# A transformer block with causal attention: softmax sums from four added key tiles instead of two, and the projection's weights loaded and gated later

## The chip, the core and the metric

The kernel runs on one core of a Trainium2 chip. The core has a matrix engine (TensorE, PE in the profile), two vector engines (VectorE, DVE; GpSimd, POOL), an engine for activation functions (ScalarE, ACT) and a queue that issues most of the loads and stores (SyncE, SP). Each engine takes its instructions in order, and waits for others by semaphores. The metric is the device time of one execution in microseconds (us), the median of some runs.

## The reference

x is 2 batch rows x 2048 tokens x 512; the condition is 2 x 512; 16 heads of 32; all in float32.

```python
mod = silu(condition) @ Wada + bada
sh_a, sc_a, gt_a, sh_m, sc_m, gt_m = split(mod, 6, axis=1)
xm = layernorm(x, g1, be1) * (1 + sc_a) + sh_a
q, k, v = split_heads(xm @ Wqkv)
scores = where(causal, q @ k.T * hd ** -0.5, -inf)
att = softmax(scores) @ v                       # per head, then merged
x = x + gt_a * (att @ Wproj + bproj)
xm = layernorm(x, g2, be2) * (1 + sc_m) + sh_m
x = x + gt_m * (gelu(xm @ W1 + b1) @ W2 + b2)
```

## The kernel before

The work goes row by row: QKV of row 0, attention of row 0, the projection of row 0 with the beginning of QKV of row 1, QKV and attention of row 1, the projection of row 1, and then the MLP over both rows.

**Units and steps.** The 16 heads are four groups c of four heads (HC = 4). A unit is one group and one block i of 512 queries: 16 units for each row, in the order i = 0, 1, 2, 3 for the first group and 0, 2, 1, 3 for the others; the last one, unit 15, is (c = 3, i = 3). A unit's steps are its key tiles of 128: 4i full steps, and then three masked ones (widths 512, 384 + 128 and 256). So a unit of i = 3 has 15 steps, one of i = 0 has 3.

**A step** (`scores_t`, L444) makes transposed scores, keys on the partitions, queries along the row, in four PSUM banks `st`, one for each head. Each bank first takes the product `st<-fold,sel`, which puts minus the row maximum into it, and then adds the product of keys and queries. ScalarE's exponential of each bank is the tile `e` (12 buffers, three steps). In a masked step GpSimd clears the upper triangle with `affine_select` (L487). Two steps later (LAG = 2) TensorE multiplies e with the values into `o` (four heads side by side, 32 columns each) and, for the softmax's denominator, with a matrix of ones into `sm`.

**Sums.** Full steps do not multiply each e with ones. GpSimd adds the e of an even and the following odd step, head by head (`pair_sums`, L504 to L508, the tiles `ee`, EE_BUFS = 6), and the set of four products with ones of that sum is put into the list `pending` for LAG + 1 = 3 steps after the odd step (L632 to L639). Masked steps multiply their e directly. `flush(now)` at the end of each step's scores emits what is due. `finish` (L517) copies o and sm, sends the sums through a reciprocal and DRAM (r, rd, rb) and multiplies (`ot` times `rb`, L540, on VectorE).

**Maxima ahead.** The row maxima must be known before a unit begins. In the same steps TensorE therefore makes the plain scores of units up to two ahead (`row.score`, tiles `s` in two PSUM banks, and once in a step a borrowed `st` bank), and VectorE reduces each tile to its maximum (L363, or L358 for masked tiles). How many tiles a step makes is paced by the cost list `weight` (L563) and the function `due` (L566). When a unit's last tile is reduced, `split` (L366) writes the maxima as a high and a low part into `mhl` (a cast at L377 and a subtraction at L378), and `rows` (L414) transposes them (`ps_m`) and makes `fold` from them. The last unit has no tiles left to make.

**Before the projection.** `prefetch` (L313), called in step 3 of the last unit, takes the buffer `kst0` of the finished keys and loads into it two blocks of attention output (`at_s`), four tiles of x (`xt_s`) and the four tiles that the next stage needs first (`next_s`). The projection's weights `wproj` and its bias `bgate` have buffers of their own. `gate_weights` (L817) loads them in the QKV stage of the same row, broadcasts the gate of the condition with one product (`rows_of`) and multiplies it into bgate and the four parts of wproj on VectorE. `project_phase` (L826) adds bgate to each tile of x on GpSimd (L849), multiplies with wproj, adds and stores.

**Order.** A scheduler places the instructions on each engine's queue by their order in the program and by when it reckons their inputs and buffers ready. Instructions wrapped in `mm`, `transpose` or `act` keep the program's order on their engine: all products, and ScalarE's work in attention. GpSimd's and VectorE's work and the loads on SP may be moved, within their dependences. A pool with `bufs` buffers hands out whichever is free.

Of the kernel before, what the change touches and what calls it, by code (L numbers as in the profile page):

```python
# [8 lines left out]
F32 = mybir.dt.float32  # L9
# [3 lines left out]
ALU = mybir.AluOpType  # L13
# [14 lines left out]
def dit_block_kernel(  # L28
# [33 lines left out]

    nc = tc.nc
# [12 lines left out]
    EE_BUFS = 6  # L76
# [66 lines left out]
    wproj = bp.tile([P, C, D], F32, tag="wproj", name="wproj")  # L143
# [62 lines left out]
    def rows_of(psum, r, b):  # L206

        ps = psum.tile([P, D], F32, tag="mm", name="ps_rows")
        g = slice(r * HD, (r + 1) * HD)
        mm(ps, pick[g, b, :], modr[g, :], start=True, stop=True)  # L210
        return ps
# [57 lines left out]
    class Row:  # L269
# [42 lines left out]

        def prefetch(self):  # L313

# [11 lines left out]
            self.next_s = [  # L326
                st[:, (3 * C + n) * QB : (3 * C + n + 1) * QB] for n in range(TQ)
            ]
            b = self.b
            nc.sync.dma_start(self.at_s[0], od[b][last_order[0]])  # L330
# [7 lines left out]
            nc.sync.dma_start(self.at_s[1], od[b][last_order[1]])  # L338

# [97 lines left out]
    def attention_phase(row):  # L437
        b, vv, kst, qst = row.b, row.vv, row.kst, row.qst
        with pool(f"att{b}") as ap, pool(
# [4 lines left out]
            def scores_t(u, step, n):  # L444
# [26 lines left out]
                for h in range(HC):  # L471
# [11 lines left out]
                    if tiles[0][0] >= i * TQ:  # L483
# [3 lines left out]
                        nc.gpsimd.affine_select(  # L487
                            d, d, pattern=[[0, len(tiles)], [1, P]],
                            compare_op=ALU.is_ge, fill=0.0,
                            base=0, channel_multiplier=-1,  # L490
# [13 lines left out]
            def pair_sums(es0, es1):  # L504
                out = new_sums()
                for h in range(HC):
                    nc.gpsimd.tensor_tensor(out[h], es0[h], es1[h], ALU.add)  # L507
                return out  # L508

# [65 lines left out]
            for u, (c, i) in enumerate(units):  # L575
# [5 lines left out]
                for n_step, tiles in enumerate(steps_of[u]):  # L581
                    last = n_step == steps - 1
                    if n_step == 0:
                        o = ps_op.tile([P, QB], F32, tag="o", name="o")
# [11 lines left out]
                    if u == len(units) - 1 and n_step == 3:  # L596
                        row.prefetch()
                    flush(now)
# [17 lines left out]
                    def row_sums(es, first, last, tiles=((0, 0),), sm=sm):  # L616
                        tile_by_tile(sm, lambda j, h: ones[:, :HD], es, tiles, first, last)

                    pending.append((now + LAG, values))
                    if n_step >= i * TQ:  # L620
# [3 lines left out]
                                lambda f=row_sums, es=es, tiles=tiles, first=n_step == 0,  # L624
                                last=last: f(es, first, last, tiles),
# [4 lines left out]
                    else:  # L630
                        ee = pair_sums(even, es)
                        pending.append(  # L632
                            (
                                now + LAG + 1,
                                lambda f=row_sums, ee=ee, first=n_step == 1: f(
                                    ee, first, False
# [710 lines left out]
```

## Time and profile before

| | us |
|---|---|
| three runs | 2582.82, 2585.14, 2586.33 |
| median | 2585.14 |
| the profiled execution | 2578.87 |
| its span in the trace | 2577.2 |
| TensorE busy | 2502.1 |
| VectorE busy | 1303.3 |
| ScalarE busy | 894.7 |
| GpSimd busy | 840.3 |

| stretch, us from the start of the span | what runs |
|---|---|
| 0 to 227 | condition and QKV of row 0 |
| 227 to 837 | attention of row 0, of which the last unit some 45 |
| 837 to 1097 | projection of row 0, QKV of row 1 |
| 1097 to 1708 | attention of row 1 |
| 1708 to 2577 | projection of row 1, MLP |

The granted TensorE clock was 0.993 over the run. In a line of groups stand the kernel's line, the engine, the operation, out<-in by the tiles' names, the shape and the count; then the busy time and the mean ns of one, and the idle time of the engine before them with what ended most of it. In a timeline each line begins with the start and the length in us, and equal neighbours are merged (x4); what stands in brackets is the engine's idle time before it and what ended that. A product in float32 shows two records, so a set of four heads' sums is x8.

### The profile page before, as it was taken

What the parts mean: (1) busy time and instruction counts of PE and PEld (TensorE: products, weight loads), DVE (VectorE), ACT (ScalarE), POOL (GpSimd) and SP (SyncE); (2) the same over time, 40 slices, a digit from 0 to 9 for tenths busy, and PEclk for the clock granted to TensorE, in tenths of its full rate; (3) what the DMA queues carried; (4) which work ended last, traced back from release to release, by engine and by line L of the source; (5) the groups of instructions that cost most, each with busy time, mean ns of one, the idle gap of its engine ahead of it and who ended that gap; (6) DMA issues with size and microseconds to landing.
All of it is one profiled execution on the core that took longest, in us unless ns stands there. A gap on an engine that the chain in (4) does not pass through costs nothing.

```text
span 2577.2 us, 31684 instructions
## 1 busy us (share of the span) xinstructions
PE 2502.1 (97%) x11361; PEld 1184.8 (46%) x11361; DVE 1303.3 (51%) x2768; ACT 894.7 (35%) x1667; POOL 840.3 (33%) x1038
## 2 busy tenths in 40 slices
PE   7999999999999999999999999999999999999998
PEld 3444444444444444544444444444444444444443
DVE  3465657657560625656565665426343344434424
ACT  1213454544445011154545444533312311311310
POOL 0001454544546266245445455543100200100100
PEclk9999999999999999999999999999999999999999
DMA  6735123242210698641422212035223332332322
GB/s 217 225 118 147 40 53 73 60 87 71 60 35 32 237 290 290 206 86 55 87 71 61 60 55 83 34 102 173 90 94 110 106 102 77 132 102 76 137 82 94
DMA packets 137991, 277.62 MB, mean 108 GB/s; under 512 B 19509, under 2 KB 48221, under 8 KB 133738
## 3 DMA queue, kind: packets, MB, share of 16 engines
q1 hardware_dynamic: 132354, 252.49, 32.8%
q0 software_dynamic: 5376, 23.07, 2.5%
q8 instruction: 89, 1.46, 0.2%
q14 instruction: 68, 0.56, 0.1%
q10 hardware_dynamic: 104, 0.05, 0.0%
HBM read 201.64 MB, written 73.66 MB: 107 GB/s over the span
## 4 chain that ended last, share of the span: by engine, by line
PE 89%; DVE 5%; DMA 4%; issue 1%; ACT 1%; SPq 0%; POOL 0%; DVEq 0%; ACTq 0%; POOLq 0%
PE st L187 18%; PE ps_h L187 15%; PE ps_y L187 15%; PE o L187 9%; PE s L187 8%; PE ps_qk L187 8%; PE sm L187 6%; PE ps_v L187 4%; PE ps_o L187 3%; DMA rb<-r 2%; DVE mx L363 2%; DVE junk L358 1%; PE ps_xt L195 1%; DMA r<-r 1%; DMA x<-in_x_dram 0%
## 5 line engine op out<-in xcount | busy, mean ns | idle before, releaser
L482 ACT ACTIVATE e<-st 128x512 f32<-128x512 f32 (+1 forms) x1152 | 575.6, 576 | 569.8 <-PE st L187 532.2
L507 POOL TENSOR_TENSOR ee<-e 128x512 f32<-128x512 f32 x384 | 485.0, 1292 | 442.1 <-ACT e L482 266.8
L363 DVE TENSOR_REDUCE mx<-s 128x1 f32<-128x512 f32 x616 | 414.0, 686 | 284.3 <-PE s L187 283.3
L187 PE MATMUL s<-kst,qst 128*128 128x512 f32 (+3 forms) x1058 | 451.6, 446 | 18.5 <-DVE mx L358 9.6
L187 PE MATMUL st<-qst,kst 128*128 128x512 f32 (+3 forms) x1280 | 435.9, 390 | 0.0
L187 PE MATMUL o<-e,vv 128*32 128x512 f32 (+3 forms) x2560 | 293.1, 539 | 0.0
L358 DVE CUSTOM_DVE_ANT_0 junk<-s,causal 128x384 bf16<-128x384 f32 (+3 forms) x442 | 211.3, 478 | 152.4 <-PE s L187 144.5
L187 PE MATMUL ps_h<-sx,w 128*128 128x512 f32 x640 | 286.7, 592 | 0.0
L187 PE MATMUL ps_y<-sh,w 128*128 128x512 f32 x640 | 276.6, 592 | 0.0
L187 PEld LDWEIGHTS st<-qst,kst 128*128 128x128 f32 x1280 | 227.8, 189 | 87.5 <-issue 63.0
L187 PEld LDWEIGHTS s<-kst,qst 128*128 128x128 f32 x1058 | 198.6, 189 | 150.3 <-DVE mx L363 54.4
L487 POOL TENSOR_SCALAR_AFFINE_SELECT e<-e 128x128 f32<-128x128 f32 (+1 forms) x384 | 125.2, 333 | 402.8 <-ACT e L482 395.8
L187 PE MATMUL ps_qk<-xmT,wqkv 128*128 128x512 f32 x512 | 243.9, 604 | 2.2 <-DVE xmT L243 2.2
L1118 POOL TENSOR_TENSOR c<-c 128x512 f32<-128x512 f32 x32 | 40.6, 1269 | 616.0 <-DVE c L1080 584.4
L1080 DVE TENSOR_TENSOR h<-c,ps_h 128x512 f32<-128x512 f32 x128 | 88.0, 688 | 231.4 <-PE ps_h L187 231.3
L187 PEld LDWEIGHTS ps_h<-sx,w 128*128 128x128 f32 x640 | 121.1, 190 | 150.2 <-issue 149.7
L187 PEld LDWEIGHTS ps_y<-sh,w 128*128 128x128 f32 x640 | 120.7, 190 | 147.8 <-issue 146.4
L187 PE MATMUL st<-fold,sel 32*128 32x512 f32 (+1 forms) x1152 | 164.4, 485 | 2.6 <-DVE mhl L378 2.2
L187 PEld LDWEIGHTS st<-fold,sel 32*128 32x128 f32 x1152 | 66.0, 183 | 197.1 <-ACT e L482 107.5
L1104 ACT ACTIVATE h<-h,cols 128x512 f32<-128x512 f32 x128 | 92.4, 722 | 181.9 <-DVE h L1080 181.9
L187 PEld LDWEIGHTS ps_qk<-xmT,wqkv 128*128 128x128 f32 x512 | 95.6, 193 | 100.6 <-issue 93.2
L187 PE MATMUL ps_v<-wqkv,xmT 128*128 128x512 f32 x256 | 122.7, 595 | 2.1 <-ACT xmT L248 2.1
(119 smaller groups left out, 2256.7 us busy)
## 6 DMA issues: line engine op xcount, KB each, us to landing
qst<-q SPq DMA_DIRECT2D x128, 256.0 KB
w<-w1d SPq DMA_DIRECT2D x34, 896.0 KB
w<-w2d SPq DMA_DIRECT2D x28, 1024.0 KB
kst<-k SPq DMA_DIRECT2D x24, 1024.0 KB
q<-hl SPq DMA_DIRECT2D x32, 512.0 KB
k<-hl SPq DMA_DIRECT2D x32, 512.0 KB
kst<-k SPq DMA_DIRECT2D x32, 256.0 KB
rb<-r SPq DMA_DIRECT2D x32, 256.0 KB
```

Of the source, the lines that this page charges most:

```text
L187: return tc.keep_in_program_order(nc.tensor.matmul(*args, **kw))
L195: return tc.keep_in_program_order(nc.tensor.transpose(dst, src, ident[:n, :n]))
L358: nc.vector.tensor_tensor_reduce(junk[:, :w], s[:, :w], causal[:, QB - w :], 1.0, MASKED, ALU.add, ALU.max, m,)
L363: nc.vector.tensor_reduce(m, s[:, :w], axis=AX.X, op=ALU.max)
L482: act(nc.scalar.activation(e[:, :w], sts[h][:, :w], AF.Exp))
L487: nc.gpsimd.affine_select(d, d, pattern=[[0, len(tiles)], [1, P]], compare_op=ALU.is_ge, fill=0.0, base=0, channel_multiplier=-1,)
L507: nc.gpsimd.tensor_tensor(out[h], es0[h], es1[h], ALU.add)
L1080: nc.vector.tensor_tensor(dst, x, y, op)
L1104: nc.scalar.activation(d, d, AF.Gelu, bias=col(r_b1 + chunk, 1))
L1118: nc.gpsimd.tensor_tensor(c1_, c1_, c2_, ALU.subtract)
```

## The change

- EE_BUFS goes from 6 to 12.
- Two neighbouring pairs' sums are added once more (`four_sums`): head 0 on VectorE, heads 1 to 3 on GpSimd, in place into the first pair's tiles. This is emitted one step after the second pair, and the one set of products with ones is due LAG + 2 steps after the second pair's odd step. `row_sums` works out for itself which set is the first of a unit.
- GpSimd's additions and `affine_select` in attention are wrapped in `act`, so they keep the program's order.
- `wproj` has no buffer of its own: it lies in the last quarter of kst0, where next_s was, and next_s takes a buffer of the query tiles (`qst`). The weights and the bias are loaded in `prefetch`, and gated in step 7 of the last unit, with the gate's product in an `s` bank.

```diff
-    EE_BUFS = 6
+    EE_BUFS = 12
...
-    wproj = bp.tile([P, C, D], F32, tag="wproj", name="wproj")
...
+        def old_queries(self):
+            t = bp.tile([P, HC, QB], F32R, tag="qst", name="qst", bufs=AHEAD + 2)
+            return t.bitcast(F32)
+
         def prefetch(self):
...
-            self.next_s = [
-                st[:, (3 * C + n) * QB : (3 * C + n + 1) * QB] for n in range(TQ)
-            ]
+            self.wproj = st[:, 3 * C * QB :].rearrange("p (c d) -> p c d", c=C)
+            t = self.old_queries()
+            self.next_s = [t[:, n, :] for n in range(TQ)]
             b = self.b
+            nc.sync.dma_start(self.wproj, Wproj.rearrange("(c p) f -> p c f", p=P))
+            nc.sync.dma_start(bgate, bproj.partition_broadcast(P))
...
+        def gate_weights(self):
+            ps = rows_of(ps_sp, 0, self.b, "s")
+            nc.vector.tensor_tensor(bgate, bgate, ps, ALU.mult)
+            for c in range(C):
+                nc.vector.tensor_tensor(
+                    self.wproj[:, c, :], self.wproj[:, c, :], ps, ALU.mult
+                )
...
-                        nc.gpsimd.affine_select(
+                        act(
+                            nc.gpsimd.affine_select(
...
-                    nc.gpsimd.tensor_tensor(out[h], es0[h], es1[h], ALU.add)
+                    act(nc.gpsimd.tensor_tensor(out[h], es0[h], es1[h], ALU.add))
                 return out
+
+            def four_sums(ee0, ee1):
+                for h in range(HC):
+                    if h == 0:
+                        nc.vector.tensor_tensor(ee0[h], ee0[h], ee1[h], ALU.add)
+                    else:
+                        act(nc.gpsimd.tensor_tensor(ee0[h], ee0[h], ee1[h], ALU.add))
...
+                    if u == len(units) - 1 and n_step == 7:
+                        row.gate_weights()
                     flush(now)
...
+                    if later:
+                        four_sums(*later)
+                        later = None
...
                         ee = pair_sums(even, es)
-                        pending.append(
-                            (
-                                now + LAG + 1,
-                                lambda f=row_sums, ee=ee, first=n_step == 1: f(
-                                    ee, first, False
-                                ),
+                        if n_step % 4 == 1:
+                            ee0 = ee
+                        else:
+                            later = ee0, ee
+                            pending.append(
+                                (now + LAG + 2, lambda f=row_sums, ee=ee0: f(ee, False))
                             )
-                        )
...
-            elif g == 2 and n == 5:
-                gate_weights(ps_mm, 0)
...
-            if g == 1 and n == 5:
-                gate_weights(ps_mm, 1)
```

More of the change, by code (lines that the diff above doesn't have):

```diff
@@ L204, in inv_std, with rows_of @@
         nc.vector.reciprocal(rstd[:, lo:hi], rstd[:, lo:hi])
-    def rows_of(psum, r, b):
-        ps = psum.tile([P, D], F32, tag="mm", name="ps_rows")
+    def rows_of(psum, r, b, tag):
+        ps = psum.tile([P, D], F32, tag=tag, name="ps_rows")
         g = slice(r * HD, (r + 1) * HD)
@@ L486, in scores_t @@
                         d = d[:, : len(tiles), :]
[L487 to L490, printed above, removed]
+                        act(
+                            nc.gpsimd.affine_select(
+                                d, d, pattern=[[0, len(tiles)], [1, P]],
+                                compare_op=ALU.is_ge, fill=0.0,
+                                base=0, channel_multiplier=-1,
+                            )
                         )
@@ L583, in attention_phase @@
                     if n_step == 0:
+                        summed, later = set(), None
                         o = ps_op.tile([P, QB], F32, tag="o", name="o")
@@ L614, in values, with row_sums @@
                         )
-                    def row_sums(es, first, last, tiles=((0, 0),), sm=sm):
+                    def row_sums(es, last, tiles=((0, 0),), sm=sm, summed=summed):
+                        first = not summed
+                        summed.add(len(summed))
                         tile_by_tile(sm, lambda j, h: ones[:, :HD], es, tiles, first, last)
+                    if later:
+                        four_sums(*later)
+                        later = None
                     pending.append((now + LAG, values))
@@ L623, in attention_phase @@
                                 now + LAG,
-                                lambda f=row_sums, es=es, tiles=tiles, first=n_step == 0,
-                                last=last: f(es, first, last, tiles),
+                                lambda f=row_sums, es=es, tiles=tiles, last=last: f(
+                                    es, last, tiles
+                                ),
                             )
@@ L815, in step @@
                 )
-    def gate_weights(psum, b):
-        nc.sync.dma_start(wproj, Wproj.rearrange("(c p) f -> p c f", p=P))
-        nc.sync.dma_start(bgate, bproj.partition_broadcast(P))
-        ps = rows_of(psum, 0, b)
-        nc.vector.tensor_tensor(bgate, bgate, ps, ALU.mult)
-        for c in range(C):
-            nc.vector.tensor_tensor(wproj[:, c, :], wproj[:, c, :], ps, ALU.mult)
     def project_phase(row, psum, between):
@@ L852, in project_phase @@
                         mm(
-                            ps, at[:, c, t * P : (t + 1) * P], wproj[:, c, :],
+                            ps, at[:, c, t * P : (t + 1) * P], row.wproj[:, c, :],
                             start=(c == 0), stop=(c == C - 1),
```

## The prediction

> **What bounds the kernel now.** I read the page first (busy shares, chain, groups), then the groups by shape, then the timeline of single engines in an attention unit with scores, in the last unit, and wherever VectorE and GpSimd worked at once.
>
> ```profile
> PE 2502.1 (97%) x11361; PEld 1184.8 (46%) x11361; DVE 1303.3 (51%) x2768; ACT 894.7 (35%) x1667; POOL 840.3 (33%) x1038
> PE 89%; DVE 5%; DMA 4%; issue 1%; ACT 1%; SPq 0%; POOL 0%; DVEq 0%; ACTq 0%; POOLq 0%
> L507 POOL TENSOR_TENSOR ee<-e 128x512 f32<-128x512 f32 x384 | 485.0, 1292 | 442.1 <-ACT e L482 266.8
> ```
>
> TensorE is the chain; GpSimd has slack on average: 384 pair adds, 485 us of two attention phases of 610 us each (227 to 837 and 1097 to 1708 us). Next, TensorE in unit 7 of the first batch row (3.6 us steps with row-maximum scores between):
>
> ```profile
> 486.43 0.50 PE L187 MATMUL st<-fold,sel 32*128 32x512 f32 x4
> ...
> 490.14 0.50 PE L187 MATMUL st<-fold,sel 32*128 32x512 f32 x4
> ...
> 492.72 1.07 PE L187 MATMUL sm<-ee,ones 128*32 128x512 f32 x8
> 493.60 1.04 PE L187 MATMUL o<-e,vv 128*32 128x512 f32 x8
> 494.57 0.50 PE L187 MATMUL st<-fold,sel 32*128 32x512 f32 x3
> ```
>
> A step begins at its fold product. The step without a sums product took 3.71 us, the next one, with it, 4.43; the set of sums (four heads) holds TensorE 493.60 - 492.72 = 0.88 us. In the last unit, which has no scores left to make, it is different:
>
> ```profile
> 791.31 1.09 PE L187 MATMUL st<-fold,sel 32*128 32x512 f32 x4
> 794.45 1.10 PE L187 MATMUL st<-fold,sel 32*128 32x512 f32 x4
> 797.61 1.09 PE L187 MATMUL st<-fold,sel 32*128 32x512 f32 x4
> 801.61 0.50 PE L187 MATMUL st<-fold,sel 32*128 32x512 f32 x4
> ```
>
> Two steps without sums take 3.14 and 3.16 us; of the following steps one with and one without take 6.56 us together (801.61 to 808.17 in the same view). So a set costs only 6.56 - 6.30 = 0.26 us there; the exponentials fill the rest. GpSimd in that unit:
>
> ```profile
> 790.46 4.99 POOL L507 TENSOR_TENSOR ee<-e 128x512 f32<-128x512 f32 x4 [6.46 <-ACT e L482]
> 796.75 2.51 POOL L507 TENSOR_TENSOR ee<-e 128x512 f32<-128x512 f32 x2 [1.31 <-ACT e L482]
> ...
> 832.25 1.12 POOL L487 TENSOR_SCALAR_AFFINE_SELECT e<-e 128x128 f32<-128x128 f32 x4 [0.62 <-ACT e L482]
> ```
>
> An add takes 4.99/4 = 1.25 us; the projection's first product followed at 837.28. Last, VectorE beside GpSimd, two timelines:
>
> ```profile
> 363.90 1.30 DVE L377 CAST mhl<-m 128x16 fp32r<-128x16 f32 x1
> 365.24 1.21 DVE L378 TENSOR_TENSOR mhl<-m,mhl 128x16 fp32r<-128x16 f32 x1
> 459.12 0.17 DVE L377 CAST mhl<-m 128x16 fp32r<-128x16 f32 x1
> 459.32 0.18 DVE L378 TENSOR_TENSOR mhl<-m,mhl 128x16 fp32r<-128x16 f32 x1
> ```
>
> ```profile
> 363.89 5.00 POOL L507 TENSOR_TENSOR ee<-e 128x512 f32<-128x512 f32 x4 [2.93 <-PE sm L187]
> 456.33 2.52 POOL L507 TENSOR_TENSOR ee<-e 128x512 f32<-128x512 f32 x2 [3.25 <-ACT e L482]
> ```
>
> The same cast and subtraction take 0.17 and 0.18 us when GpSimd rests (459) and 1.30 and 1.21 us when adds run (364): each lasted to the end of the add that had begun before it. ot times rb behaves likewise: 0.69 us alone, up to 1.72 beside adds, and the add behind it grows from 1.25 to 1.70.
>
> **The change, part by part.** Each term is microseconds of the whole run; minus is gained.
>
> *Sums products removed.* Pairs per unit are 0, 2, 4 and 6 for 0, 4, 8 and 12 full steps: 12 pairs for one head group, times 4 groups and 2 rows = 96 sets; 48 go. Six of them lie in the two last units, which I cost apart. The other 42 lie mostly in steps with scores: 42 x 0.88 = **-37**. Ends: if some 12 of them (the scoreless ends of units 3, 7, 11, 14) are worth 0.26, -30; if every set also spares a stall, some 1.0 each by the mean difference of steps with and without (4.83 against 3.90 over the scored steps), -42.
>
> *GpSimd in the last unit.* In the built order its queue now holds there: pairs 1 and 2, three adds of the four, pairs 3 and 4, three adds, then the four xt + bgate adds of the projection (before, between two units with GpSimd idle), pairs 5 and 6, a mask, three adds, two masks. In time of the old run: the first pair ends at 795.5, the second starts at 796.75 as before, and from there it never rests: 20 pair adds + 9 + 4 = 33 x 1.25 = 41.3, masks 3.7, and some 1.6 of growth where VectorE cuts in: end at 843.3 instead of 833.4. What is queued behind: pair 5 starts 5 us late, and the exponentials of step 11 need the e buffers it reads, so TensorE's step 12 starts late too; the sums and values of the last two steps wait for the masks. After the mask before last, near 842.2, TensorE has three sets of 0.86: 844.9 against 837.28, +7.6 a row, **+15**. Ends: +5 if the bgate adds ran elsewhere and the masks overtook; +20 with a further stall of the buffers.
>
> *VectorE's add.* 48 new adds of two SBUF operands. No row shows it; nearest is ot times rb, 0.69 us free and up to 1.72 beside adds. [...] Mean excess over the gap 0.3, of which two or three score banks absorb a part: 0.2 each for the 28 that lie in steps with scores = **+6** (0 to +21). It waits for the first add of the second pair; behind it are queued the maxima, and behind those TensorE's scores. In the last unit VectorE is idle (1.1 us busy of 46), so there it costs nothing but GpSimd's growth.
>
> *Old VectorE work that now meets adds.* Before, the second pair's last two adds waited for sums products (64 waits, 175 us), so GpSimd rested when the maxima were split; with 12 buffers it does not. Unit 6 at 459: the new add waits to 458.8 and ends at 459.4, the cast waits to 460.5, the subtraction to 461.8; the following maxima come 1.3 us late, in a step where TensorE's transpose already waits 0.9 for VectorE. Units 6 and 10, both rows: 4 x 1.3; unit 2 by the same count 2 x 1.7; unit 14, 2 x 1.2: **+11** (0 to +20). ot times rb in units 3, 7, 11 meets the adds of four: 6 x 0.4 = **+2** (0 to +6).
>
> *The gate.* One product (0.55 us) and five VectorE multiplies (5 x 0.68) leave each QKV stage, where TensorE shows one gap of 0.30 at 153.2: **-2** (0 to -4). They land in the last unit's eighth step, with VectorE idle; the weights are ready some 5 us before GpSimd wants bgate. The 1 MB load goes out when the old keys are released (first loads at 687.7), 12 us ahead of the next stores of sums (699.6); before the rb load of unit 11 stand as many x loads as before. New on SP's queue is a wait for unit 12's query buffer, whose last reader ran near 701, before SP gets there (703): **+1** (0 to +8, since the rb load, VectorE's product and the maxima stand behind it). bgate's load moves too, hidden by tens of microseconds.
>
> Sum: -37 + 15 + 6 + 11 + 2 - 2 + 1 = **-4**. The profiled execution took 2578.9 us, so 2575; the median of the three runs is 2585.1, 6.3 us above it: **2581**.
>
> [...] The rows show waits that end with the running add, whenever that began, so I keep 0.2.
>
> **Rivals.**
> - *Collisions fall into gaps.* The mean of VectorE is 343 us busy of 610 per phase, and every wait for GpSimd vanishes under it: -37 - 2 + 15 + 5 = -19, 2566. Against it: the transposes that already wait on VectorE.
> - *VectorE passes GpSimd's waits on to TensorE* (the one that ends slower). Place: the step boundaries with a new add. [...] It decides from 0.33 us an add; from 0.52 the run is measurably slower. For it: casts of 1.3 us; against it: 1 us gaps.
> - *GpSimd or SP holds more than the last unit.* In a 12-step unit GpSimd needs 33 x 1.25 + 5 = 46 us of 60.5 (482.64 to 542.95), so it should not; were the four-step rhythm (14.3 us) late, or rb held by SP, some 1.5 us in each of 16 units more: +20, 2605.
> - *The sums products don't go*: excluded, the built program has 48 sets fewer.
>
> **How the numbers follow.** The sum as worked out (-12 to +5) 0.40; collisions hidden 0.25; passed on 0.27; held 0.08. A measurement tells about 0.2%, 5.2 us, from no change. Of the first case 0.17 is beyond -5.2; with the second, faster 0.42; same 0.22; slower 0.36. The range takes in -21 to +23: 2564 to 2608; the likeliest case's own is 2573 to 2590.
>
> **What would show it.** 384 instead of 768 TensorE records of the sums from added tiles, with steps without them still near 3.6 us; last units 7 to 8 us longer, GpSimd without rest from their fourth step; casts of 1.3 us in units 6 and 10; VectorE adds of 0.6 to 1.8 us. Wrong if steps of the scored units get longer by more than 0.5 us where such an add stands, or if the last unit ends near its old length.

## The result, and the profile after

The changed kernel takes 2609.2 us (median of 2606.2 to 2622.8), the kernel before 2584.0 us beside it: the ratio is 1.0108, 95% interval 1.0070 to 1.0146. It is slower, by 25 to 28 us, where 2581 us was predicted; the time lies 1 us outside the range given (2564 to 2608). The profiled execution took 2606.4 us.

From the page of the changed kernel: span, TensorE's share, GpSimd's, the chain of waits, and the group of the pair adds.

```profile
span 2604.6 us, 31031 instructions
PE 2492.6 (96%) x10977; PEld 1187.0 (46%) x10977; DVE 1380.6 (53%) x2816; ACT 898.7 (35%) x1667; POOL 1041.5 (40%) x1182
PE 83%; DVE 7%; DMA 6%; POOL 3%; issue 1%; ACT 1%; SPq 0%; DVEq 0%; ACTq 0%; POOLq 0%
L526 POOL TENSOR_TENSOR ee<-e 128x512 f32<-128x512 f32 x384 | 504.9, 1349 | 324.9 <-ACT e L499 324.9
```

TensorE has 11361 - 10977 = 384 products less, as the change says, but is busy only 9.5 us less in a span that is 27.4 us longer: its products have got longer on average (those of values, `o`, 128x512, from 603 to 626 ns). And it carries 83% of the chain, not 89%; VectorE, the DMAs and GpSimd have taken over the rest. The mean clock granted to TensorE tells the same (last line of the view of clocks; before, then changed):

```profile
core 0: 2577.2 us, clock 0.993
```

```profile
core 0: 2604.6 us, clock 0.982
```

0.011 of 2600 us is 29 us more of missing clock, as large as the whole loss. The prediction has no term for it.

**Where the time went, step by step.** A step runs from its four fold products to the next four. I took the start of all 288 steps of both traces, and for each step the time in which no product ran ("idle"). Of the 27.4 us, the beginning (the QKV stage without the gate) gives -3.9; the steps outside the two last units +9.7; the steps of the last units +18.0 (up to the start of their last step, whose own length changes by 0.4 us or less); the projection and QKV between the rows +3.5. The +9.7 in its turn is 44 sets of sums less (42, and one in each row that now falls into the first step of the last unit), at 0.865 us each -38.1, then +25.5 of idle time, and +22.3 of steps that are longer without being idle. Most steps behave as predicted: one that loses its set is 0.86 shorter, one that gets a set 0.86 longer, the others are equal within 0.02. The loss sits in some 30 steps. Two places show its kinds.

*First kind: the multiplication `ot` times `rb`, with the maxima behind it.* VectorE in the changed kernel's unit 3 of row 0, and the same place before:

```profile
330.80 1.01 DVE L532 TENSOR_TENSOR ee<-ee 128x512 f32<-128x512 f32 x1
334.39 1.57 DVE L566 TENSOR_TENSOR ot<-ot,rb 128x512 f32<-128x512 f32 x1 [2.58 <-DMA rb<-r]
335.88 0.68 DVE L380 TENSOR_REDUCE mx<-s 128x1 f32<-128x512 f32 x1
```

```profile
336.30 0.69 DVE L540 TENSOR_TENSOR ot<-ot,rb 128x512 f32<-128x512 f32 x1 [1.96 <-DMA rb<-r]
```

TensorE meanwhile waits for a score bank that the maxima behind the multiplication must free; changed, then before:

```profile
336.62 0.50 PE L187 MATMUL s<-kst,qst 128*128 128x512 f32 x1 [3.45 <-DVE mx L380]
```

```profile
337.65 0.50 PE L187 MATMUL s<-kst,qst 128*128 128x512 f32 x1 [1.03 <-DVE mx L363]
```

ScalarE's copy of the sums, which starts the chain of DMAs to `rb`, ended at 324.33 in the changed kernel and at 327.79 before. TensorE comes to the place 8.8 us after it in both. The multiplication starts 10.06 us after it instead of 8.51, because rb arrives later, and takes 1.57 instead of 0.69, because GpSimd is adding: 1.55 + 0.88 = 2.43, and TensorE's gap grows by 3.45 - 1.03 = 2.42. So VectorE's waits pass through to TensorE in full here. Over all 32 units (view of the tile `ot`: minimum, median and maximum of one in ns; before, then changed):

```profile
L540 DVE TENSOR_TENSOR ot<-ot,rb x32: 689/693/1721, 299.9 to 1718.1; 128x512 f32<-128x512 f32 x32
```

```profile
L566 DVE TENSOR_TENSOR ot<-ot,rb x32: 679/1141/1653, 298.6 to 1745.9; 128x512 f32<-128x512 f32 x32
```

The exception has become the rule: the median multiplication now meets an add.

*Second kind: two short gaps, and a slow clock behind them.* VectorE and then TensorE in unit 6 of row 0 of the changed kernel:

```profile
455.16 0.93 DVE L394 CAST mhl<-m 128x16 fp32r<-128x16 f32 x1
456.34 0.98 DVE L395 TENSOR_TENSOR mhl<-m,mhl 128x16 fp32r<-128x16 f32 x1
```

```profile
457.85 0.39 PE L187 MATMUL s<-kst,qst 128*128 128x256 f32 x1 [1.05 <-DVE mx L375]
459.14 0.33 PE L195 MATMUL ps_m<-ident,mhl 128*128 128x128 f32 x1 [0.90 <-DVE mx L375]
459.40 1.06 PE L187 MATMUL o<-e,vv 128*32 128x512 f32 x8
...
460.77 0.80 PE L187 MATMUL st<-fold,sel 32*128 32x512 f32 x4
...
465.53 1.94 PE L187 MATMUL o<-e,vv 128*32 128x512 f32 x8
```

The cast and the subtraction take 0.93 and 0.98 instead of 0.17 and 0.18; that they meet adds in this unit was predicted. The new thing is a gap of 1.05 in front of the 0.90 that was there before, and what follows: the same eight products of values take 1.06 us at 459.40 and 1.94 at 465.53. The step from 460.77 is idle for no moment and takes 6.62 us where it took 3.87. The stretches before and after 460 (columns: stretch, length, busy time and count of PE, PEld, DVE, ACT, POOL, granted clock, DMA share, GB/s):

```profile
453.00:460.00 7.00, 5.05 (x31) 2.17 (x29) 6.57 (x21) 2.27 (x5) 7.00 (x10) 1.00 0.40 114
460.00:467.00 7.00, 7.00 (x34) 4.07 (x26) 4.76 (x14) 2.39 (x4) 3.62 (x6) 0.55 0.26 78
```

The granted clock fell to a half. In the trace's clock records it does so for 3.4 or 6.8 us at a time (5.5 and 5.8 at the very end): 36 us in all before, 95 us in the changed kernel; in the attention outside the last units 20 us before and 68 changed. At half clock the 48 us between them are worth up to 24, about the +22.3 of steps that are longer without being idle.

*The last unit* is in the main as predicted; it took 52.0 us before (785.32 to 837.28) and takes 61.1 in both rows now. GpSimd there (row 0), TensorE's fold products in the step from 830.83, and VectorE's third new add:

```profile
800.31 5.44 POOL L526 TENSOR_TENSOR ee<-e 128x512 f32<-128x512 f32 x4 [1.30 <-ACT e L499]
...
823.96 4.97 POOL L876 TENSOR_TENSOR kst<-kst,bgate 128x512 f32<-128x512 f32 x4
828.90 9.84 POOL L526 TENSOR_TENSOR ee<-e 128x512 f32<-128x512 f32 x8
...
843.42 2.97 POOL L505 TENSOR_SCALAR_AFFINE_SELECT e<-e 128x256 f32<-128x256 f32 x8
```

```profile
830.83 0.50 PE L187 MATMUL st<-fold,sel 32*128 32x512 f32 x1 [2.29 <-ACT e L499]
832.06 0.50 PE L187 MATMUL st<-fold,sel 32*128 32x512 f32 x1 [0.73 <-ACT e L499]
```

```profile
835.07 10.41 DVE L532 TENSOR_TENSOR ee<-ee 128x512 f32<-128x512 f32 x1 [14.20 <-POOL ee L526]
```

GpSimd works from 800.31 to 846.39 without rest, 46.1 us (46.6 predicted); the banks wait for exponentials, which wait for buffers of e that GpSimd still has to read. The clock falls to a half at 832.8 for 6.8 us, and so it does in row 1, at 1720.2.

VectorE's third new add of the unit took 10.41 us, in both rows. The prediction had such an add wait for the running add of GpSimd and then take its turn (0.6 to 1.8 us in all), and so do the first two of this unit, with 1.75 and 1.77. Here GpSimd began and ended 13 further instructions while the add lasted. TensorE waited 0.19 us for it in row 0.

### The profile page after: what moved, and what is told of

Its sections match the earlier page's. It is cut to its first block, busy times and chain, and to the rows that moved or that the text cites. A ratio compares the mean times of both kernels' runs of the same rounds, so it can differ in the third digit from the quotient of the medians.

```text
span 2604.6 us, 31031 instructions
## 1 busy us (share of the span) xinstructions
PE 2492.6 (96%) x10977; PEld 1187.0 (46%) x10977; DVE 1380.6 (53%) x2816; ACT 898.7 (35%) x1667; POOL 1041.5 (40%) x1182
## 4 chain that ended last, share of the span: by engine, by line
PE 83%; DVE 7%; DMA 6%; POOL 3%; issue 1%; ACT 1%; SPq 0%; DVEq 0%; ACTq 0%; POOLq 0%
PE st L187 16%; PE ps_h L187 15%; PE ps_y L187 15%; PE o L187 9%; PE s L187 8%; PE ps_qk L187 7%; PE sm L187 4%; PE ps_v L187 4%; PE ps_o L187 3%; DMA rb<-r 3%; DVE mx L380 2%; POOL ee L526 2%; DVE junk L375 1%; PE ps_xt L195 1%; DMA r<-r 1%
## 5 line engine op out<-in xcount | busy, mean ns | idle before, releaser
L526 POOL TENSOR_TENSOR ee<-e 128x512 f32<-128x512 f32 x384 | 504.9, 1349 | 324.9 <-ACT e L499 324.9
L187 PE MATMUL s<-kst,qst 128*128 128x512 f32 (+3 forms) x1058 | 456.9, 451 | 31.7 <-DVE mx L375 21.4
L187 PE MATMUL st<-qst,kst 128*128 128x512 f32 (+3 forms) x1280 | 446.4, 399 | 0.0
L187 PE MATMUL o<-e,vv 128*32 128x512 f32 (+3 forms) x2560 | 302.2, 554 | 0.0
L187 PEld LDWEIGHTS st<-qst,kst 128*128 128x128 f32 x1280 | 236.1, 197 | 90.1 <-issue 65.1
L187 PE MATMUL st<-fold,sel 32*128 32x512 f32 (+1 forms) x1152 | 173.8, 494 | 17.9 <-ACT e L499 8.6
L534 POOL TENSOR_TENSOR ee<-ee 128x512 f32<-128x512 f32 x144 | 184.8, 1312 | 0.0
```

Of the source, the lines that this page charges most:

```text
L187: return tc.keep_in_program_order(nc.tensor.matmul(*args, **kw))
L526: act(nc.gpsimd.tensor_tensor(out[h], es0[h], es1[h], ALU.add))
L534: act(nc.gpsimd.tensor_tensor(ee0[h], ee0[h], ee1[h], ALU.add))
```

## The experiments

Units are counted from 0 here; the expectations on record say "third unit" for unit 2, and so on. The changed kernel was not run again beside the experiments. Each has runs of the kernel before beside it, so it is the ratios to the kernel before that are compared; 0.001 is 2.6 us. Behind each ratio stands what the trace gives for the steps outside the last units, as above (idle time, and longer without being idle, both against the kernel before; the changed kernel has +25.5 and +22.3), and for the last units (changed: +18.0).

**The gate and Wproj alone** (sums from pairs, six buffers; GpSimd's work stays in the program's order), written as an edit of the changed kernel:

```diff
-    EE_BUFS = 12
+    EE_BUFS = 6
...
-                        if n_step % 4 == 1:
-                            ee0 = ee
-                        else:
-                            later = ee0, ee
-                            pending.append(
-                                (now + LAG + 2, lambda f=row_sums, ee=ee0: f(ee, False))
-                            )
+                        pending.append(
+                            (now + LAG + 1, lambda f=row_sums, ee=ee: f(ee, False))
+                        )
```

> The kernel before with the move of the gate and of Wproj alone: sums from pairs, six buffers. If the sums from four tiles (their adds and what they delay) make the loss: like the kernel before, 2577 to 2590 us; the attention starts some 4 us earlier, and the last unit of a row is longer by the two to three us of the gate's step. If the moved load or gate holds SyncE or the last unit: 2600 or more.

Measured: 2591.9 us, 1.0062 (1.0046 to 1.0078). Outside the last units nothing happens (idle +0.6, rest +0.5): neither SyncE's new wait nor the load cost anything to speak of there. The last units are 8.7 us longer, 4.3 in each row. Of these, 3.7 to 3.9 are one step in which the banks wait for exponentials, behind the four adds of xt and bgate that stand in the middle of GpSimd's queue:

```profile
805.21 5.00 POOL L526 TENSOR_TENSOR ee<-e 128x512 f32<-128x512 f32 x4 [1.11 <-PE sm L187]
810.15 5.01 POOL L871 TENSOR_TENSOR kst<-kst,bgate 128x512 f32<-128x512 f32 x4
```

Neither expectation held quite: it lies between. The move is a loss by itself, and by the trace these adds are the place. The whole difference of the two traces is 9.9 us, where the ratio says 16.

**Pairs in the last unit** of each row; the rest as changed:

```diff
-                        if n_step % 4 == 1:
+                        if u == len(units) - 1:
+                            pending.append(
+                                (now + LAG + 1, lambda f=row_sums, ee=ee: f(ee, False))
+                            )
+                        elif n_step % 4 == 1:
```

> The changed kernel with pairs only in the last unit of each row. If GpSimd's queue in the last unit makes the loss: the two last units get 9 to 11 us shorter each, 2587 to 2591, which is about the time before. If the rest, VectorE's waits in the other units with the slow clock behind them, makes as much: the same gain here, and 2587 to 2591 still does not reach the 2566 to 2570 that the removed sums products should then give. If the last unit's length comes from the gate's step: under 5 us gained.

Measured: 2593.6 us, 1.0072 (1.0051 to 1.0093), so some 9 us better (14 in the trace), where 18 to 22 had been expected. The last units are +3.8 instead of +18.0, the others much as in the changed kernel (idle +18.9, rest +26.1). The last unit is a part of the loss, and the smaller one.

**No add on VectorE**:

```diff
-                    if h == 0:
-                        nc.vector.tensor_tensor(ee0[h], ee0[h], ee1[h], ALU.add)
-                    else:
-                        act(nc.gpsimd.tensor_tensor(ee0[h], ee0[h], ee1[h], ALU.add))
+                    act(nc.gpsimd.tensor_tensor(ee0[h], ee0[h], ee1[h], ALU.add))
```

> The changed kernel with all four adds of a group on GpSimd, none on VectorE. If VectorE's 48 new adds are what delays the maxima: 6 us or more faster, 2603 or less. If it is VectorE's old work (ot times rb, the split of the maxima) meeting GpSimd's adds: GpSimd is busier by 48 x 1.28 = 61 us, so the same or slower, 2605 to 2625; the last units longer by up to 3 us each.

Measured: 2611.8 us, 1.0140 (1.0125 to 1.0155), not better. Taking VectorE's 48 new adds away gains nothing. As GpSimd gets them instead and is busier, this run alone does not clear them; the steps of the changed kernel do: 30 of the 42 outside the last units in which such an add stands differ by 0.03 us or less from the kernel before, apart from their set.

**ot times rb on GpSimd**:

```diff
-                nc.vector.tensor_tensor(ot, ot, rb, ALU.mult)
+                nc.gpsimd.tensor_tensor(ot, ot, rb, ALU.mult)
```

> The changed kernel with ot times rb on GpSimd, so that VectorE's maxima no longer stand behind it. If the maxima behind ot times rb (waiting for the DMA of rb, then for GpSimd) make most of the stalls outside the last units: the stalls at these places go with the slow clock behind them, 15 to 30 us gained, 2580 to 2595. If the loss lies in GpSimd's load or in the last units alone: 32 x 1.25 us more for GpSimd, 2609 or more.

Measured: 2932.1 us, 1.1374 (1.1343 to 1.1405). The first expectation is missed. The time is over the 2609 of the second, but by far more than its 32 x 1.25 = 40 us and for another reason. From the view of waits:

```profile
POOL ot L566 <- DMA rb<-r: 434.3, 23, 25.1
ACT e L499 <- POOL ee L526: 292.0, 103, 12.0
```

GpSimd now stood still for rb, 434 us in 23 waits, with the adds and masks behind it that free the buffers of e. It moves the wait to an engine with more behind it, and tells nothing on the question; it shows what an in-order wait for this DMA can cost.

**ot times rb later in VectorE's order.** The multiplication is handed on four steps later and kept in program order there:

```diff
-                nc.vector.tensor_tensor(ot, ot, rb, ALU.mult)
-                nc.sync.dma_start(od[b][i][:, c, :], ot)
+                def scale():
+                    act(nc.vector.tensor_tensor(ot, ot, rb, ALU.mult))
+                    nc.sync.dma_start(od[b][i][:, c, :], ot)
+
+                pending.append((now + 4, scale))
+                pending.sort(key=lambda p: p[0])
...
-            flush(now + LAG)
+            flush(now + LAG + 6)
```

> The changed kernel with ot times rb four steps further back in VectorE's order (it moves in five units of each row, the third, seventh, eleventh, twelfth and thirteenth, where VectorE stood idle for the DMA of rb). If the DMA of rb, with the maxima behind it, is what the shorter steps laid bare: the stalls at those ten places (19.8 us of TensorE idle in the changed kernel, about 7 before) go with the slow clock behind some, 10 to 20 us gained, 1.003 to 1.007 of the kernel before. If GpSimd's adds stretch VectorE's work instead: under 5 us gained, 1.009 to 1.012.

Measured: 2583.5 us, 1.0024 (1.0011 to 1.0038): 0.0084 or 22 us gained, a little more than the first theory's range, from a move that only concerns ten of 32 multiplications. The idle time falls from +25.5 to +3.1, the rest stays (+21.7). VectorE and TensorE at the place that was shown above:

```profile
342.15 1.56 DVE L568 TENSOR_TENSOR ot<-ot,rb 128x512 f32<-128x512 f32 x1
343.64 0.68 DVE L380 TENSOR_REDUCE mx<-s 128x1 f32<-128x512 f32 x1
```

```profile
337.01 0.39 PE L187 MATMUL s<-kst,qst 128*128 128x512 f32 x1
```

The multiplication still meets an add and takes 1.56 us, but finds rb there, and TensorE does not wait: the step takes 3.57 us instead of 7.46. 0.9 us of stretch is absorbed by the score banks; 0.9 on top of 2.6 us of waiting is not.

**The adds of xt and bgate behind the last unit** (kept in program order):

```diff
-                    nc.gpsimd.tensor_tensor(xt, xt, bgate, ALU.add)
+                    act(nc.gpsimd.tensor_tensor(xt, xt, bgate, ALU.add))
```

> The changed kernel with the four adds of xt and bgate kept behind the last unit's work on GpSimd. If GpSimd's queue makes the last unit long: 4 x 1.25 = 5 us less in each last unit and part of the slow clock there, 8 to 14 us gained in both, 1.005 to 1.008 of the kernel before. If the projection then waits for these adds instead: 0 to 3 us gained.

Measured: 2600.6 us, 1.0091 (1.0068 to 1.0114). The last units fall from +18.0 to +4.5 in the trace, and the profiled run was the fastest of the four (2594.2); the median gains only 4 us, and the interval overlaps that of the changed kernel. The +4.5 leave out the units' last step, which is 1.1 us longer than before in row 0 and 4.3 in row 1. In row 1 TensorE waits there for VectorE's third new add, which took 10.95 us beside GpSimd's work, and half clock follows:

```profile
1718.06 1.81 PE L187 MATMUL sm<-ee,ones 128*32 128x512 f32 x8 [2.38 <-DVE ee L532]
```

The place is right, the gain by itself is not settled.

**Sets of zeros in the place of the removed sets.** 48 times four products of zeros are added to `sm` where the removed sets stood, on keys, so that they wait for no add; the values stay the same:

```diff
+    zeros = bp.tile([P, HD], F32, tag="zeros", name="zeros")
+    nc.gpsimd.memset(zeros, 0.0)
...
+                    def empty_sums(sm=sm, summed=summed, k=kst[c]):
+                        first = not summed
+                        summed.add(len(summed))
+                        products(
+                            sm, lambda h: zeros, [k[:, h, :].bitcast(F32) for h in range(HC)], 0, 0,
+                            first, False,
+                        )
...
                         if n_step % 4 == 1:
                             ee0 = ee
+                            pending.append((now + LAG + 1, empty_sums))
```

> The changed kernel with 48 sets of products of zeros added to the sums, where the removed sets stood and with nothing to wait for: TensorE has its old work again, GpSimd and VectorE the new. If the 37 us of removed products were gained and the loss stands beside it: about 35 us slower than the changed kernel, 1.022 to 1.027 of the kernel before. If the products were only cover for waits that are now bare, with a slow clock behind: 0 to 15 us slower, or even faster, 1.008 to 1.016.

Measured: 2637.3 us, 1.0229 (1.0201 to 1.0257), 0.0121 or 31 us slower than the changed kernel. The removed products were really gained; the loss stands beside them, it is not the same time laid bare.

**Three mends together** (multiplication later, adds of bgate behind, pairs in the last unit), the three edits of above in one:

```diff
+                    act(nc.vector.tensor_tensor(ot, ot, rb, ALU.mult))
...
+                pending.append((now + 4, scale))
...
+                        if u == len(units) - 1:
...
+                    act(nc.gpsimd.tensor_tensor(xt, xt, bgate, ALU.add))
```

> The changed kernel with three mends: ot times rb four steps later, xt + bgate behind the last unit, pairs alone in the last unit. If the three are the loss and add up: 10 to 20, 8 to 14 and 10 less the overlap of the last two, 25 to 38 us gained, 0.996 to 1.001 of the kernel before. If the casts and ot times rb beside GpSimd's adds with the slow clock make the rest: 15 to 25 us gained, 1.001 to 1.005.

Measured: 2575.7 us, 0.9995 (0.9982 to 1.0008). 29 us gained, as the first expectation had it, which brings the change back to no change. Idle +7.5, rest +18.1, last units +2.6. The rest, with its slow clock, was still there.

**The split of the maxima on GpSimd**, on top of the three mends:

```diff
-            nc.vector.tensor_copy(hl[:, :, :, 0], m)
-            nc.vector.tensor_tensor(
+            nc.gpsimd.tensor_copy(hl[:, :, :, 0], m)
+            nc.gpsimd.tensor_tensor(
```

> The three mends, and the cast and the subtraction that split the maxima done on GpSimd itself, so that VectorE no longer waits for GpSimd there. If these two are what still empties TensorE in the units of four and eight full steps (two gaps of 1.05 and 0.90 us in the third, seventh, eleventh and fifteenth unit, each with half the clock for 6.8 us behind): 12 to 20 us less than the three mends, 0.992 to 0.995 of the kernel before. If the split then comes too late in GpSimd's queue for TensorE's transposes: 1.000 to 1.006.

Measured: 2577.8 us, 0.9986 (0.9973 to 1.0000), no better within the intervals. Idle +8.2, rest +24.8. GpSimd waits for the maximum with its adds and masks behind (5.08 us in unit 6), and TensorE's idle time in that step is 3.36 instead of 1.89.

**Eight buffers for the added tiles**, on top of the three mends:

```diff
-    EE_BUFS = 12
+    EE_BUFS = 8
```

> The three mends with eight buffers for the added tiles instead of twelve. If GpSimd's rest, forced by few buffers, is what kept the split of the maxima free of adds in the kernel before: the casts are short again and 8 to 16 us go, 0.993 to 0.997 of the kernel before. If GpSimd runs the adds of the second pair at the same time all the same: like the three mends, 0.998 to 1.001.

Measured: 2584.5 us, 1.0015 (1.0001 to 1.0029), if anything worse: idle +18.0, rest +25.0. Fewer buffers do not give VectorE its quiet moment back; the casts of units 6 and 10 still take 0.93 us.

**The kernel before with ot times rb four steps later**, nothing else:

```diff
-                nc.vector.tensor_tensor(ot, ot, rb, ALU.mult)
...
+                    act(nc.vector.tensor_tensor(ot, ot, rb, ALU.mult))
...
+                pending.append((now + 4, scale))
...
```

> The kernel before with nothing but ot times rb four steps later. If the wait for the DMA of rb is bare in the kernel before as well, only shorter: TensorE's idle time at the five places (about 7 us in both rows, and 7 us of half clock) goes, 4 to 10 us gained, 0.996 to 0.9985 of the kernel before. If the longer steps cover it: 0.9985 to 1.001.

Measured: 2573.7 us, 0.9971 (0.9961 to 0.9981), 7 us gained. The wait was bare before too, at a third of its price.

**ot times rb eight steps later after units 5, 9 and 13**, on top of the three mends:

```diff
-                pending.append((now + 4, scale))
+                pending.append((now + (8 if i == 2 and c else 4), scale))
```

> The three mends with ot times rb eight steps later after the sixth and tenth unit, where it now meets GpSimd's adds (1.4 us instead of 0.69) in front of TensorE's transpose (1.86 us of idle time against 0.5 before). If that meeting matters: four stalls of 1.3 us go with some slow clock, 5 to 10 us less than the three mends, 0.9955 to 0.998 of the kernel before. If the multiplication meets adds wherever it stands: 0.999 to 1.001.

Measured: 2565.0 us, 0.9936 (0.9915 to 0.9957), 15 us less than the three mends, more than expected. The four stalls of 1.8 us behind units 5 and 9 are 0.5 again; the idle time falls from +7.5 to -1.9 and the rest from +18.1 to +13.2. The edit also moves the multiplication of unit 13, which the expectation does not mention: out of unit 14, where it waited 0.6 and 1.5 us for rb, into the last unit. Unit 14 gets 3.2 and 1.0 us shorter in the two rows, so the 15 us are not those four stalls alone.

**The transpose behind the products of values**, on top of that. In the steps that are not a unit's last, TensorE first makes the products of values of two steps ago and then the transpose that waits for the split:

```diff
-                        if last or (ready > u + 1 and n_step >= 1):
+                        early = last or (ready > u + 1 and n_step >= 1)
+                        if last:
                             row.rows(u + 1)
+                    else:
+                        early = False
...
                     flush(now)
+                    if early and not last:
+                        row.rows(u + 1)
```

> The later multiplication (three mends, ot times rb four and eight steps later) with TensorE's transpose of the split maxima put behind the step's products of values instead of in front. If two gaps close together (1.05 us for a score bank, 0.90 us for the transpose) are what sets the clock to a half: one of the two is filled, the clock stays up in the third, seventh, eleventh and fifteenth unit, 5 to 10 us of idle time and 10 to 13 us of slow clock go, 0.984 to 0.989 of the kernel before. If the transpose, and so the fold, then comes too late for the next unit: 0.9935 to 1.000.

Measured: 2536.0 us, 0.9823 (0.9801 to 0.9844), better than the better expectation and faster than both kernels, 45 us under the kernel before. Idle is 11.7 us under the kernel before, the rest 0.8 under it: most slow steps are gone (17 us of half clock outside the last units, 51 without this move, 20 in the kernel before). The place of the second kind in this kernel, TensorE and the stretches around it:

```profile
451.59 0.39 PE L187 MATMUL s<-kst,qst 128*128 128x256 f32 x1 [1.05 <-DVE mx L375]
451.90 1.06 PE L187 MATMUL o<-e,vv 128*32 128x512 f32 x8
452.90 0.33 PE L195 MATMUL ps_m<-ident,mhl 128*128 128x128 f32 x1
...
457.35 1.06 PE L187 MATMUL o<-e,vv 128*32 128x512 f32 x8
```

```profile
446.00:453.00 7.00, 5.95 (x34) 2.46 (x33) 6.57 (x21) 3.00 (x6) 7.00 (x9) 1.00 0.41 102
453.00:460.00 7.00, 6.19 (x39) 3.82 (x39) 5.80 (x20) 3.06 (x7) 5.05 (x9) 1.00 0.28 83
```

The first gap of 1.05 us is the same to the hundredth. The second is filled by products; TensorE is busy 5.95 of 7 us instead of 5.05, the clock stays full, and the next eight products take 1.06 us, not 1.94. It does not help everywhere. Before the move half clock stands at five of the eight places of this kind (units 2, 6, 10 and 14 of both rows), with it at two. One is the same place in unit 10 of row 0:

```profile
602.46:605.87 3.41, 2.13 (x16) 0.70 (x15) 2.98 (x10) 0.54 (x2) 3.41 (x7) 1.00 0.42 114
605.87:612.70 6.83, 6.83 (x30) 4.09 (x29) 3.96 (x14) 2.39 (x4) 3.51 (x6) 0.50 0.24 69
```

There a gap of 1.05 us and one of 0.23 were enough. That the two gaps make the half clock is thus the likely cause, by count, and not a rule for the single place.

**The kernel before with both moves of order** (multiplication later, transpose behind), sums from pairs; the edits are those of above:

```diff
+                pending.append((now + (8 if i == 2 and c else 4), scale))
...
+                    if early and not last:
+                        row.rows(u + 1)
```

> The kernel before, sums from pairs, with the same two moves of order (ot times rb later, transpose behind the products). If the two moves help the kernel before about as much as they help the changed one: 0.988 to 0.993 of the kernel before, and the sums from four tiles bring little beyond. If its stalls were short and its clock full anyway: 0.994 to 0.998, and the sums from four tiles are then worth the difference to the run above.

Measured: 2556.5 us, 0.9908 (0.9891 to 0.9925). The time lies in the range of the first expectation, but its reading does not hold: the sums from four tiles do bring something beyond. From the kernel before with the late multiplication (0.9971) the step is 0.0063, 16 us (the eight steps for units 5, 9 and 13 included); the transpose's move in the changed kernel with its mends, 0.9936 to 0.9823, is 29 us. The idle time that goes is not larger there (9.8 us against 15.4); the 14 us that the rest loses there are what differs, and these are the slow clock (half clock outside the last units: 51 to 17 us there, 31 to 27 here). Between the two kernels with both moves, the sums from four tiles, with the gate's move and pairs in the last units, are worth 0.0085 or 22 us.

**A late split without GpSimd**, in the kernel with the gate alone, for the units of twelve full steps:

```diff
+            if units[u][1] == 3:
+                wide = bp.tile([P, HC * TQ, 32], F32, tag="wide", name="wide")
+                nc.vector.tensor_copy(wide, m.unsqueeze(2).to_broadcast([P, HC * TQ, 32]))
+                m = bp.tile([P, HC * TQ], F32, tag="m2", name="m2")
+                nc.vector.tensor_reduce(m, wide, axis=AX.X, op=ALU.max)
             m = m.rearrange("p (h t) -> p h t", h=HC)
```

> The move of the gate alone (1.0062 of the kernel before), with the split of the maxima of the units of twelve full steps made about 1.0 to 1.4 us late by two operations of VectorE (copy to 128x512 and maximum of it, the values stay the same): four places in each row, no add of GpSimd in play. If a late split costs its length alone: 8 x 1.2 = 10 us, 1.009 to 1.011. If the two gaps set the clock to a half for 3.4 to 6.8 us each time: 8 x (1.2 + 1.7 to 3.4) = 23 to 37 us, 1.015 to 1.021, and half clock is seen at these eight places.

Measured: 2605.7 us, 1.0093 (1.0078 to 1.0108), 8 us more than the gate alone. Of the eight places six cost 0.4 us or less each, less than the length of the two operations. Two, in unit 14 of each row, got 3.5 and 2.9 us longer. The time agrees with the first expectation, and half clock follows at two of the eight places alone. Where TensorE's gap before the transpose grew long, the clock did fall (unit 14 of row 0):

```profile
782.45 0.33 PE L195 MATMUL ps_m<-ident,mhl 128*128 128x128 f32 x1 [3.29 <-DVE mhl L400]
...
784.18 1.95 PE L187 MATMUL o<-e,vv 128*32 128x512 f32 x8
```

```profile
783.00:786.40 3.40, 3.40 (x20) 0.73 (x12) 0.64 (x1) 0.00 (x0) 1.86 (x2) 0.50 0.70 224
```

So a late split is not dear by itself; it is where it makes a long gap. The two gaps close together did not arise in this run (in unit 6 of row 0 they were 0.20 and 0.91 us), so it tells nothing on them.

## Why the prediction was wrong

By its own steps, in the order of the sum (-37 + 15 + 6 + 11 + 2 - 2 + 1 = -4; measured +25 to +28):

- *Sums products removed, -37*: right. 44 sets left the steps outside the last units, 0.865 us each; putting sets of zeros back cost 31 us, with six sets in the cheap last units. (The 4.83 and 3.90 us behind the end of -42 do not come out of the trace before, which gives 4.79 and 4.10 for the steps outside the last units.)
- *GpSimd in the last unit, +15*: right in mechanism (46.1 us without rest, the adds of bgate in the middle, exponentials waiting for buffers), a little small: +18.0 in the steps, 1.7 of them the two sets that moved in from unit 14. What it lacked is the half clock behind the stall in each row.
- *VectorE's new adds, +6*: right that they are no great cost, and still too much. Most steps with such an add are unchanged to 0.03 us, and without them the kernel is not faster. The excess of 0.3 us that the term takes is one over VectorE's gap (1.06 us up to 491.34 in unit 7 of the kernel before); it and the +21 at the term's end rest on the author's estimate of an add by itself, which no run shows: the shortest adds take 0.67 to 0.69 us. And the two of 10.41 us show that such an add need not wait for one running add only.
- *Old VectorE work that now meets adds, +11*: right in units 2, 6 and 10 with the lengths (0.93 and 0.98 us in unit 6), but wrong in price. The prediction let 1.3 to 1.7 us a place pass through to TensorE, 8.6 us for these six places. The steps with the split and behind it cost 21.6 us beyond the sets: in unit 6 of row 0, +1.4 in the step with the gaps and +2.8 in the next one. Other steps of these units got 6.5 us shorter, so that the units lost 15.1 as a whole. The mis-sized part is what follows the wait, the half clock, and it was missing from every term. In unit 14 (2.4 us predicted, 8.5 beyond the sets) the casts stayed short, and the multiplication, 1.22 us beside an add, took their part.
- *ot times rb, +2 (0 to +6)*: **this is the step that failed first.** It counted six multiplications that meet adds of four at 0.4 us. It overlooked that this multiplication waits for a chain of DMAs with nothing to spare, that the maxima stand behind it, and that the median multiplication would meet an add. Moving ten of them gave 22 us, moving six (units 5, 9 and 13) further another 15.
- *The gate, -2*: not settled. The beginning got 3.9 us shorter, but up to 1.7 of that is a half clock of 3.4 instead of 6.8 us at 20 us from the start, and the stretch between the rows, where the gate of row 1 had stood, got 3.5 longer. Its adds on GpSimd were in the term of the last unit; alone the move costs 0.0062 or 16 us, 9.9 in its trace; the terms hold 9 for it (10 for eight adds of 1.25, -2 and +1).
- *SP, +1 (0 to +8)*: right; with the gate alone the units 13, where the new wait stands, are 0.4 and 0.8 us longer.

The rival "VectorE passes GpSimd's waits on to TensorE" had the right end (slower) and the right chain, but at the wrong instruction: at the new adds, which are harmless. "Collisions fall into gaps" is true of those adds, and false of the multiplication. "GpSimd or SP holds more than the last unit" did not happen: with the gate alone nothing outside the last units changed, and in unit 7 of the changed kernel GpSimd still rests 4.04, 1.98 and 1.03 us between its adds. (That unit took 60.3 us before, by the two times that the prediction gives for it, not 60.5.) Of the signs named in advance, the 384 products and the unrested GpSimd came as said, the casts shorter (0.93 instead of 1.3 us), the last units longer by 9 us instead of 7 to 8, and 46 of VectorE's 48 adds within 0.6 to 1.8 us; the sign for being wrong, steps longer by more than 0.5 us, came too, though mostly in steps where `ot` times `rb` or a split stands.

Beside GpSimd's adds in the changed kernel the multiplication takes up to 1.65 instead of 0.69 us and the subtraction behind the cast up to 0.98 instead of 0.18; the maxima take 0.63 to 0.69 throughout, beside adds too. The adds of 10.41 us lasted over many instructions of GpSimd, not one. Why, no run shows. What the prediction got wrong is where it looked for the price: at the new adds, which cost next to nothing in the scored units, instead of the multiplication.

What stays open: how the 22.3 us of longer steps divide between single places in other executions. Of like places in the two rows some had the half clock and some not (unit 10: in row 1, not in row 0), and the four runs of the changed kernel spread over 16 us, the slowest with the lowest clock (0.973). And in the gain of the adds of bgate alone the interval is too wide.

## What to carry to other kernels

A wait is priced by what is queued behind it. Before giving an engine more work, list the instructions on its neighbours that already wait for something late (here one multiplication behind a chain of DMAs) and see whether they still have room; moving such instructions back in their queue was worth 37 us in two runs, as much as the products that the change removed. Where TensorE stalls, add up the gaps within a few microseconds, not each alone: a slow clock behind them can cost as much again as the gaps (here +22.3 us beside +25.5 of idle time), and products put into one of them can save both (29 us here), if not at every place. And a change that loses may be good on a kernel whose waits are covered: with the two moves of order, the sums from four tiles gain 22 us, and the whole is 45 us faster than the kernel before.

## What the hardware showed that was not expected

The granted clock of TensorE falls to exactly half (0.50), for 3.4 or 6.8 us (10.2 at three places of the run with the multiplication eight steps later), after gaps that are short: 1.05 and 0.90 us with 0.4 us of work between. In the changed kernel's trace there are 17 falls, the last of them 5.8 us long, up to the end; at 16 of them TensorE had been busy for 13 to 64% of the 3.41 us before, worked out from the rows of its products, and the other one came at the start of the attention behind a busy stretch. Stretches of 44 to 64% did not always lead to a fall. The 3.42 us in front of the fall at 460.7 were 57% busy. The 33 changes of the clock in this trace all lie on one grid of 3.413 us, to 0.001 us. That it matters how gaps lie on that grid is the author's reading; no run tests it alone. Unit 10 of row 0 has the same two gaps, 1.05 and 0.90 us, but in two stretches of the grid, 68 and 75% busy, and its clock stayed full (the stretches of unit 6 with the fall, then those of unit 10):

```profile
457.28:460.70 3.42, 1.95 (x11) 0.67 (x11) 2.69 (x10) 0.00 (x0) 3.42 (x7) 1.00 0.27 87
460.70:467.53 6.83, 6.83 (x30) 4.02 (x29) 4.36 (x13) 2.39 (x4) 2.92 (x6) 0.50 0.27 79
610.88:614.30 3.42, 2.31 (x9) 1.16 (x7) 3.28 (x11) 2.08 (x4) 3.42 (x7) 1.00 0.52 140
614.30:617.71 3.41, 2.57 (x17) 1.18 (x18) 2.64 (x10) 0.00 (x0) 3.41 (x3) 1.00 0.24 60
```
